# The last tile of scores in PSUM banks of its own, and the last output in half chunks over two queues

## The chip, the cores and the metric

One core of one Trainium2 chip runs the whole kernel. The metric is device time in microseconds (us), from start to end of one execution. The kernel before took 549.41 us (median of 3 runs, 548.23 to 549.83).

In the profile's rows PE is the matrix engine (PEld its weight loads), DVE the vector engine, ACT the scalar engine, POOL the GpSimd engine, and SP the engine that does nothing but issue transfers. SPq and ACTq are the sequencers that issue DMA transfers for SP and ACT.

## The reference

A graph attention layer over 16 graphs of 512 nodes with 512 features. `v` holds the nodes, `q` a condition vector per graph, `adj` an integer mask with 11 labels. Cut to what matters:

```python
vcq = concat([v, q_exp], -1)                   # q_exp is 0 in rows whose sum is 0
self_feat = vcq @ W_self.T + b_self            # 16 x 512 x 512
output = self_feat
for d in range(2):                             # the mask, and the mask transposed
    A = (adj if d == 0 else swapaxes(adj, 1, 2))[:, :, :20]
    bias = A @ w_bias + b_bias                 # 512 nodes x 20 keys
    qh, kh = heads(self_feat @ Wq[d].T + bq[d]), heads(self_feat[:, :20] @ Wk[d].T + bk[d])
    aff = where(A.sum(-1) > 0, qh . kh / sqrt(32), NEG) + bias     # 16 heads
    w = softmax(aff, -1)                       # over the 20 keys
    out_t = einsum('bnhm,bmf->bnhf', w, self_feat[:, :20])
    output += einsum('bnhf,hgf->bnhg', out_t, Wout[d]) + bout[d]
return v + relu(output)
```

Everything is float32. The kernel holds node features transposed, features on the partitions and nodes along the columns, and returns `out` as 16 x 512 features x 512 nodes; the host turns it back.

## The kernel before, in words

**Stages.** A setup (keys, folded weights, values) is followed by one round per graph, b = 0 to 15. The order of all instructions is written out by hand, and each engine runs its own in that order. A round computes the self features of the next graph, the scores of this one, and the output of the one before, so PE always has something to do. The last graph has no successor, and its work is written out below the loop: this is the tail, from about 515 us on, and only its last 10 us change.

**Scores.** For one graph there are four tiles of scores, (c, l): l is the half of the nodes (256 of them), c says which heads. A tile has 4 groups of 64 nodes, and for each group 4 heads x 40 numbers (2 directions x 20 keys) on each of two halves of the partitions. The last tile is (1, 1). It is computed in two parts, i = 0 and 1, of two groups each, so that the softmax of part 0 runs while PE computes part 1. Part i has a PSUM bank of its own, `ps_e0` or `ps_e1`. A part goes through: maximum and subtraction (DVE, `weigh_plain`, L463 and L465), exponential (ACT, L468), sum and reciprocal (DVE, `total_part`, L474 and L475), multiplication by the reciprocal (`normal_part`, L479; part 0 on POOL, part 1 on DVE) and a transposition in blocks of 32 (`turn_part`, L482, DVE) into `wt`, from where PE multiplies it with the values.

**Output.** The output of a graph gathers in four PSUM banks, `outsum[b][0..3]`. The 512 output features are four chunks of 128: chunk 2p + c. Banks 2p and 2p + 1 hold chunks 2p (c = 0, columns 0 to 255) and 2p + 1 (c = 1, columns 256 to 511); of the nodes the first of the two banks has the even blocks of 32, the second the odd ones. Banks 0 and 1 are one tile (`ps_o15_s1`), banks 2 and 3 another (`ps_o15_s0`). They start with the self features (`seed_out`, ACT, L556), and `attend` (L569) adds weights x values with `start=False`. A span (c, lo, hi) of `attend` names the half of the columns and the groups lo to hi - 1 of the 8 groups of 64 nodes; for each span and bank there are 6 matmuls, 4 with 32 and 2 with 64 output rows. Spans with c = 0 need only the tiles (0, 0) and (0, 1); (1, 0, 4) needs the tile (1, 0); (1, 4, 6) needs part 0 of the last tile, and (1, 6, 8) part 1.

`end` turns a chunk into output: relu and the node features `x` added. On DVE one instruction per bank does both (L611, 128 x 256); on ACT it is the relu alone (L613, 128 x 512 for both banks), and `add_rows` (L619) adds `x` on POOL or DVE. `send` (L1362) stores a chunk, 128 rows of 2 KB, 256 KB. An engine waits for the last instruction that another engine has, ahead in the code, on the same tile, even where the two touch different columns.

**The end of the tail before.** After `attend` of all (0, 0, 8) and of (1, 0, 4) in banks 0 and 1, ACT does the relu of chunks 2 and 0 (c = 0). POOL adds `x` to chunk 2, SP stores it. PE goes on with (1, 0, 6) in banks 2 and 3 and (1, 4, 6) in banks 0 and 1. DVE finishes part 1 of the last tile, then adds `x` to chunk 0, SP stores it. PE does (1, 6, 8) in all banks, and then DVE does `end` of chunks 3 and 1, each stored whole by SP. The reciprocals of part 1 are written into unused columns of `ps_e1`, a PSUM bank.

Of the kernel before, what the change touches and what calls it, by code (L numbers as in the profile page):

```python
# [7 lines left out]
F32 = mybir.dt.float32  # L8
# [5 lines left out]
P = 128  # L14
# [4 lines left out]
def gat_kernel(  # L19
# [449 lines left out]

    def total_part(b, c, l, i):  # L470
        f = weighs[b, c, l][:, bass.ts(i, 2)].rearrange("p g (h m) -> p (g h) m", m=NG)
        sm = soft.tile([P, per // 2], F32, tag="sm", name=f"sm{b}_{c}{l}{i}")
        smalls[i] = terms[c, l][i][:, 0, bass.ds(HL * S, per // 2)] if i else sm
        nc.vector.tensor_reduce(sm, f, AX.X, ALU.add)  # L474
        nc.vector.reciprocal(smalls[i], sm)  # L475

    def normal_part(b, c, l, i, engine):
        f = weighs[b, c, l][:, bass.ts(i, 2)].rearrange("p g (h m) -> p (g h) m", m=NG)
# [78 lines left out]
            outsum[b][a].rearrange("p (c n r) -> p c n r", c=2, r=R), spread_out(sfs[b], a), AF.Copy  # L557
        )

    def attend(b, spans=((0, 0, 2 * HL), (1, 0, 2 * HL)), banks=range(HL)):  # L560


        vd = vds[b].rearrange("p c e i g -> p c (e i g)")
        pairs, ones = ((1, 2, 1), (5, 2, 3)), ((0, 1, 0), (3, 1, 2), (4, 1, 2), (7, 1, 4))
        runs = (ones, spans[:1]), (pairs, spans), (ones, spans[1:])
        for c, lo, hi, at, n, j in [(*span, *of) for group, those in runs for span in those for of in group]:
            for a in banks:
                r = bass.ts(a, R)
                nc.tensor.matmul(  # L569
                    outsum[b][a][bass.ds(at // 2 * DH, n * DH), bass.ds(c * N // 2 + lo * R, (hi - lo) * R)].rearrange(  # L570
                        "p (n r) -> p n r", r=R
                    ),
                    vd[r, c, bass.ds(at * DH, n * DH)],
                    wts[b][r, c].rearrange("p l (g w) -> p (l g) w", g=HL)[:, lo:hi, bass.ts(j, 32)],
                    start=False, stop=n == 1 + (c == 0), skip_group_check=True,
                )
# [26 lines left out]
    def end(b, p, c, engine, us=slice(0, 2)):  # L603
# [5 lines left out]
        if engine is nc.vector:  # L609
            for u in range(us.stop - us.start):  # L610
                nc.vector.scalar_tensor_tensor(to[:, u], ps[:, u], 0.0, of[:, u], ALU.max, ALU.add)  # L611
        elif engine is nc.scalar:
            nc.scalar.activation(to, ps, AF.Relu)  # L613
        else:
            engine.tensor_add(to, to, of)

    def add_rows(b, p, c, engine):
        to = outt[b][:, 2 * p + c]
        engine.tensor_add(to, to, xs[b][:, 2 * p + c])  # L619

    def store(b, cs, ins=None):
        for c in cs:
            behind(nc.sync.dma_start(out[b, bass.ts(c, P)], outt[b][:, c]), ins)
# [451 lines left out]
    with tc.manual_schedule():  # L1075
# [275 lines left out]
        normal_part(b, 1, 1, 0, nc.gpsimd)  # L1351
        add_rows(o, 1, 1, nc.gpsimd)
        store(o, (3,))
        weigh_plain(b, 1, 1, 1)
        turn_part(b, 1, 1, 0)
        attend(b, ((0, 0, 8),))
        attend(b, ((1, 0, 4),), range(2))
        spare = const.tile([P, C, WD], F32, tag="g", name=f"o{b}", bufs=1).rearrange("p c w -> p (c w)")
        outt[b] = spare[:, : C * N].rearrange("p (c n) -> p c n", c=C)

        def send(queue, c):
            queue.dma_start(out[b, bass.ts(c, P)], outt[b][:, c])  # L1362

        for p in (1, 0):
            end(b, p, 0, nc.scalar)
        add_rows(b, 1, 0, nc.gpsimd)
        send(nc.sync, 2)
        attend(b, ((1, 0, 6),), range(2, 4))
        attend(b, ((1, 4, 6),), range(2))
        total_part(b, 1, 1, 1)  # L1370
        normal_part(b, 1, 1, 1, nc.vector)
        turn_part(b, 1, 1, 1)
        add_rows(b, 0, 0, nc.vector)
        send(nc.sync, 0)
        attend(b, ((1, 6, 8),))
        for p in (1, 0):
            end(b, p, 1, nc.vector)
            send(nc.sync, 2 * p + 1)


# [44 lines left out]
```

## Time and profile before

| | |
|---|---|
| time, median of 3 | 549.41 us |
| time of the profiled execution | 548.23 us |
| its span, first to last instruction | 546.2 us |
| busy in the span: PE, DVE, ACT, POOL | 99%, 88%, 74%, 80% |
| last matmul ends | 541.37 us |
| last DVE instruction ends | 542.82 us |
| last store issued | 542.84 us |
| DMA engines fall idle | 544.4 us |

2.0 us of the time lie outside the span. A row of the timeline has start and duration in us, engine, line and operation, output <- input with shapes, and in brackets for how long the engine was idle before and who ended that. Rows that follow each other are merged (x2). A row of stage windows has the stretch in us, its length, the busy time of PE, PEld, DVE, ACT and POOL with counts, then the granted PE clock, the busy share of the 16 DMA engines, and GB/s. In the profile each float32 matmul stands as two records.

### The profile page before, as it was taken

The numbers are of one execution on the slowest core, as the hardware profiler recorded it, in microseconds if no ns is written. First come the engines' busy times: TensorE is split into PE (matmuls) and PEld (weight loads), VectorE is DVE, ScalarE is ACT, GpSimd is POOL, SyncE is SP. The second block draws the span as 40 slices with busy tenths as digits, with TensorE's granted clock in tenths as the row PEclk, the third lists the DMA queues.
The fourth block names the chain that finished last, engine by engine and source line by source line (L and its number), as shares of the span: only waits on it lengthen the run. The fifth ranks groups of instructions, "written<-read, shape, count | busy, mean of one in ns | idle before, by whom it ended". The sixth has DMA issues, their size and how long they took to land.

```text
span 546.2 us, 19673 instructions
## 1 busy us (share of the span) xinstructions
PE 540.2 (99%) x7932; PEld 423.7 (78%) x7932; DVE 481.3 (88%) x711; ACT 404.1 (74%) x999; POOL 434.3 (80%) x418
## 2 busy tenths in 40 slices
PE   9999999999999999999999999999999999999996
PEld 6544368889888878787888878887878788878784
DVE  1776678889999999999989999999999999999997
ACT  1225435888887979788888888888878787978664
POOL 2637996779979797979798888888897979797664
PEclk9999999999999999999999999999999999999998
DMA  8999999978886877878776758676777777736034
GB/s 306 377 396 355 314 360 342 311 259 251 226 255 190 250 194 225 227 217 233 220 219 192 236 180 232 203 231 188 231 210 210 194 230 191 240 92 200 2 116 156
DMA packets 100546, 126.45 MB, mean 232 GB/s; under 512 B 19608, under 2 KB 68694, under 8 KB 98408
## 3 DMA queue, kind: packets, MB, share of 16 engines
q1 hardware_dynamic: 98856, 122.19, 72.2%
q0 software_dynamic: 1168, 2.23, 1.8%
q8 instruction: 62, 1.02, 0.8%
q10 hardware_dynamic: 432, 0.79, 0.4%
q14 instruction: 28, 0.23, 0.1%
HBM read 86.23 MB, written 40.24 MB: 232 GB/s over the span
## 4 chain that ended last, share of the span: by engine, by line
PE 97%; DVE 2%; ACT 0%; issue 0%; DVEq 0%
PE ps_f L667 32%; PE ps_a L397 24%; PE ps_c L397 11%; PE ps_d L397 6%; PE ps_o_f L569 5%; PE ps_v L893 3%; PE ps_k L831 3%; PE ps_kv L781 2%; PE ps_a L284 1%; PE ps_o_c L569 1%; PE ps_l L397 1%; PE ps_c L284 1%; PE ps_warm L737 1%; PE ps_o_s L569 0%; DVE o L611 0%; DVE w L465 0%
## 5 line engine op out<-in xcount | busy, mean ns | idle before, releaser
L327 ACT ACTIVATE prod<-adj,wb_sb 128x80 f32<-128x80 int32 x330 | 116.0, 429 | 0.0
L537 POOL TENSOR_TENSOR w<-w,sm 128x640 f32<-128x640 f32 x63 | 80.3, 1275 | 33.0 <-DVE sm L533 29.3
L667 PE MATMUL ps_f<-t,ws_s 128*64 128x246 f32 x720 | 80.0, 370 | 0.0
L667 PEld LDWEIGHTS ps_f<-t,ws_s 128*64 128x64 f32 x720 | 51.7, 136 | 18.9
L528 ACT ACTIVATE w<-w 128x640 f32<-128x640 f32 x60 | 43.9, 731 | 18.0 <-DVE w L524 18.0
L545 DVE STREAM_TRANSPOSE wt<-w 128x640 f32<-128x640 f32 x63 | 52.5, 834 | 0.1
L667 PE MATMUL ps_f<-x,ws_v 128*64 128x246 f32 x480 | 52.4, 371 | 0.0
L532 DVE TENSOR_REDUCE sm<-w 128x32 f32<-128x640 f32 x63 | 51.1, 811 | 1.1 <-ACT w L528 0.8
L523 DVE TENSOR_REDUCE ps_d<-w 128x32 f32<-128x640 f32 x59 | 48.7, 826 | 1.8 <-ACT ps_d L431 0.2
L524 DVE TENSOR_TENSOR w<-w,ps_d 128x640 f32<-128x640 f32 x59 | 48.4, 821 | 2.0
L370 POOL TENSOR_TENSOR k<-g,k 128x608 f32<-128x608 f32 x30 | 44.8, 1492 | 0.0
L667 PEld LDWEIGHTS ps_f<-x,ws_v 128*64 128x64 f32 x480 | 34.7, 137 | 13.0
L397 PEld LDWEIGHTS ps_a<-g,sf 128*64 128x64 f32 x544 | 34.2, 137 | 5.9 <-issue 5.8
L397 PE MATMUL ps_a<-g,sf 128*64 128x152 f32 x544 | 38.6, 295 | 0.0
L397 PE MATMUL ps_d<-g,sf 128*64 128x152 f32 x544 | 37.9, 293 | 0.0
L346 ACT COPY both<-add 64x80 f32<-64x80 f32 x128 | 32.6, 254 | 5.7 <-DVE add L338 4.6
L569 PE MATMUL ps_o_c<-wt,vd 32*32 32x256 f32 (+1 forms) x720 | 36.8, 386 | 0.0
L338 DVE TENSOR_REDUCE add<-prod 128x80 f32<-128x960 f32 x32 | 36.7, 1146 | 0.0
L682 POOL TENSOR_TENSOR t<-x,t 128x492 f32<-128x492 f32 x30 | 34.9, 1163 | 1.2
L397 PEld LDWEIGHTS ps_d<-g,sf 128*64 128x64 f32 x544 | 35.3, 137 | 0.2 <-ACT sf L685 0.2
L333 POOL TENSOR_SCALAR prod<-cond 128x80 f32<-128x80 f32 x32 | 18.1, 566 | 21.7 <-DVE cond L332 20.2
L569 PE MATMUL ps_o_f<-wt,vd 32*32 32x256 f32 (+1 forms) x672 | 34.6, 386 | 0.0
(300 smaller groups left out, 1435.8 us busy)
## 6 DMA issues: line engine op xcount, KB each, us to landing
g<-g_d SPq DMA_DIRECT2D x60, 304.0 KB
g_d<-st SPq DMA_DIRECT2D x16, 1064.0 KB
out_T<-o SPq DMA_DIRECT2D x64, 256.0 KB
x<-in_xT SPq DMA_DIRECT2D x56, 256.0 KB
xn<-in_xn SPq DMA_DIRECT2D x48, 256.0 KB
adj<-in_adj SPq DMA_DIRECT2D x52, 220.0 KB
vd<-bd_d SPq DMA_DIRECT2D x64, 64.0 KB
nz<-nz_d SPq DMA_DIRECT2D x14, 256.0 KB
```

The lines of the kernel that those rows point to most:

```text
L327: nc.scalar.activation(p[:, :, l], a[:, :, l], AF.Identity, scale=wb_sb[:, l : l + 1])
L338: done["masks"] = nc.vector.tensor_reduce(add, prods.pop((b, h)), AX.X, ALU.add)
L370: done["ksum"] = engine.tensor_sub(to, one, two)
L397: nc.tensor.matmul(slot(g)[bass.ts(p, P // 2), : HL * S].rearrange("p (h m) -> p h m", m=NG)[:, :, 1:], of(k)[:, bass.ds(first + g * P // ...
L523: nc.vector.tensor_reduce(mx, f, AX.X, ALU.max)
L524: done["weigh"] = (engine or nc.vector).tensor_sub(f, f, mx.unsqueeze(2).to_broadcast([P, per, NG]))
L528: done["exp"] = nc.scalar.activation(t, t, AF.Exp)
L532: nc.vector.tensor_reduce(sm, heads(weighs[b, c, l]), AX.X, ALU.add)
L537: done["normal"] = nc.gpsimd.tensor_mul(f, f, smalls.pop((b, c, l)).unsqueeze(2).to_broadcast([P, per, NG]))
L545: done["turn"] = nc.vector.transpose(wts[b][:, c, l], weighs.pop((b, c, l)).rearrange("p g w -> p (g w)"))
L569: nc.tensor.matmul(outsum[b][a][bass.ds(at // 2 * DH, n * DH), bass.ds(c * N // 2 + lo * R, (hi - lo) * R)].rearrange("p (n r) -> p n r", ...
L667: nc.tensor.matmul(parts[b][n in (2, 3, 5)][bass.ts(a, P // 2), bass.ts(i, HN)], lhs, x[:, k], start=False, stop=k == 1, skip_group_check= ...
```

## The change

Only the end of the tail changes (the line numbers after it shift by up to 21).

- Three further PSUM tiles, four banks, are taken for the last graph: `c` (two banks), `f0` and `f1`. `f0` and `f1` are the banks in which parts 0 and 1 of the last tile of scores lay. In each, the 128 columns of c = 1 and groups 4 to 7 are seeded with self features (`seed_groups`, ACT, L620, four instructions of 128 x 128), three ahead of the exponential of part 1 and one behind it.
- The spans (1, 4, 6) and (1, 6, 8) go to these banks (`base=HL`), for all four banks at a time. All of (1, 0, 4) now goes with (0, 0, 8) in one call of `attend`, ahead of ACT's relu.
- Since `f1` is the bank `ps_e1`, the reciprocals of part 1 no longer go there: they stay in SBUF (`sm`).
- `x` is added to chunk 0 on POOL, behind chunk 2, and no longer on DVE.
- Chunks 3 and 1 are finished in halves of 256 nodes (`end_groups`, DVE, L625, eight instructions of 128 x 128 in place of four of 128 x 256): groups 0 to 3 from the old banks, groups 4 to 7 from the new ones.
- Six stores in place of four. ACT's queue: the first half of 3, the first half of 1, the second half of 1. SP's queue: chunk 2 whole, the second half of 3, chunk 0 whole. A half is 128 rows of 1 KB.

```diff
     def total_part(b, c, l, i):
-        sm = soft.tile([P, per // 2], F32, tag="sm", name=f"sm{b}_{c}{l}{i}")
-        smalls[i] = terms[c, l][i][:, 0, bass.ds(HL * S, per // 2)] if i else sm
+        sm = smalls[i] = soft.tile([P, per // 2], F32, tag="sm", name=f"sm{b}_{c}{l}{i}")
         nc.vector.tensor_reduce(sm, f, AX.X, ALU.add)
-        nc.vector.reciprocal(smalls[i], sm)
+        nc.vector.reciprocal(sm, sm)
...
-    def attend(b, spans=((0, 0, 2 * HL), (1, 0, 2 * HL)), banks=range(HL)):
+    def attend(b, spans=((0, 0, 2 * HL), (1, 0, 2 * HL)), banks=range(HL), first=0, base=0):
...
-        runs = (ones, spans[:1]), (pairs, spans), (ones, spans[1:])
+        runs = ((ones, spans[:1]), (pairs, spans), (ones, spans[1:]), (ones, spans[:1]))[first : first + 3]
...
+    def columns(bank, c, lo, hi):
+        return bank[:, bass.ds(c * N // 2 + lo * R, (hi - lo) * R)].rearrange("p (n r) -> p n r", r=R)
+
+    def seed_groups(b, a, c, lo, hi):
+        nc.scalar.activation(
+            columns(outsum[b][HL + a], c, lo, hi), spread_out(sfs[b], a)[:, c, lo:hi], AF.Copy
+        )
+
+    def end_groups(b, a, c, lo, hi, bank):
+        nc.vector.scalar_tensor_tensor(
+            spread_out(outt[b], a)[:, c, lo:hi], columns(bank, c, lo, hi), 0.0, spread_out(xs[b], a)[:, c, lo:hi],
+            ALU.max, ALU.add,
+        )
...
+        new_outs(b, ((accs, "c"), (accs, "f0")))
+        for a in range(3):
+            seed_groups(b, a, 1, 4, 8)
         weigh_plain(b, 1, 1, 1)
+        new_outs(b, ((accs, "f1"),))
+        seed_groups(b, 3, 1, 4, 8)
         turn_part(b, 1, 1, 0)
-        attend(b, ((0, 0, 8),))
-        attend(b, ((1, 0, 4),), range(2))
...
+        attend(b, ((0, 0, 8), (1, 0, 4)))
         for p in (1, 0):
             end(b, p, 0, nc.scalar)
         add_rows(b, 1, 0, nc.gpsimd)
-        send(nc.sync, 2)
-        attend(b, ((1, 0, 6),), range(2, 4))
-        attend(b, ((1, 4, 6),), range(2))
+        add_rows(b, 0, 0, nc.gpsimd)
+        attend(b, ((1, 4, 6),), base=HL)
         total_part(b, 1, 1, 1)
         normal_part(b, 1, 1, 1, nc.vector)
         turn_part(b, 1, 1, 1)
-        add_rows(b, 0, 0, nc.vector)
+        attend(b, ((1, 6, 8),), first=1, base=HL)
+        send(nc.sync, 2)
+        for p in (1, 0):
+            for a in (2 * p, 2 * p + 1):
+                end_groups(b, a, 1, 0, 4, outsum[b][a])
+            send(nc.scalar, 2 * p + 1, slice(0, N // 2))
+        for p, queue in ((1, nc.sync), (0, nc.scalar)):
+            for a in (2 * p, 2 * p + 1):
+                end_groups(b, a, 1, 4, 8, outsum[b][HL + a])
+            send(queue, 2 * p + 1, slice(N // 2, N))
         send(nc.sync, 0)
-        attend(b, ((1, 6, 8),))
-        for p in (1, 0):
-            end(b, p, 1, nc.vector)
-            send(nc.sync, 2 * p + 1)
```

How the instructions stand on three engines. `o15` is the last graph's output tile, `sf15` its self features, `x15` its node features; in brackets are the engines (or DMA semaphores) whose work an instruction waits for.

ACT from the last seed of the old banks on, before:

```order
L556 ACTIVATE ps_o15_s0_7398<-sf15_6856 128x512 [waits Activation_49]
L468 ACTIVATE w15_11_7421<-w15_11_7421 128x320 [waits DVE_49]
L613 ACTIVATE o15_7475<-ps_o15_s0_7398 128x2x8x32 [waits DMAHW0_49,PE_49,Activation_49]
L613 ACTIVATE o15_7475<-ps_o15_s1_7384 128x2x8x32 [waits PE_49]
L1421 UNCONDITIONAL_BRANCH
```

and now:

```order
L555 ACTIVATE ps_o15_s0_7398<-sf15_6856 128x512 [waits Activation_49]
L620 ACTIVATE ps_o15_c_7434<-sf15_6856 128x128 [waits Activation_49] x2
L620 ACTIVATE ps_o15_f0_7435<-sf15_6856 128x128 [waits PE_49]
L468 ACTIVATE w15_11_7421<-w15_11_7421 128x320 [waits DVE_49]
L620 ACTIVATE ps_o15_f1_7443<-sf15_6856 128x128 [waits PE_49]
L612 ACTIVATE o15_7446<-ps_o15_s0_7398 128x2x8x32 [waits DMAHW0_49,PE_49]
L612 ACTIVATE o15_7446<-ps_o15_s1_7384 128x2x8x32
L1378 DMA out_T<-o15_7446 128x256 [waits DMAHW7_49,DVE_49]
L1378 DMA out_T<-o15_7446 128x256 [waits DMAHW0_49,DVE_49]
L1378 DMA out_T<-o15_7446 128x256 [waits DMAHW3_49,DVE_49]
```

Four seeds came in around the exponential L468 and three stores behind the relus. The first relu's wait for PE was for the 24th matmul of the tail's `attend` (the last one of (0, 0, 8)); since (1, 0, 4) for all banks now stands in the same call, it is for the 48th.

DVE from the reciprocal of part 1 on, before:

```order
L475 RECIPROCAL ps_e1_7306<-sm15_111_7504 128x16 [waits DVE_49]
L479 TENSOR_TENSOR w15_11_7421<-w15_11_7421,ps_e1_7306 128x320 [waits DVE_49]
L482 STREAM_TRANSPOSE wt15_7357<-w15_11_7421 128x320 [waits DVE_49]
L619 TENSOR_TENSOR o15_7475<-o15_7475,x15_6526 128x512 [waits DMAHW0_49,Activation_49]
L611 SCALAR_TENSOR_TENSOR o15_7475<-ps_o15_s0_7398,x15_6526 128x8x32 [waits PE_49]
L611 SCALAR_TENSOR_TENSOR o15_7475<-ps_o15_s0_7398,x15_6526 128x8x32
L611 SCALAR_TENSOR_TENSOR o15_7475<-ps_o15_s1_7384,x15_6526 128x8x32 x2
```

and now:

```order
L474 RECIPROCAL sm15_111_7523<-sm15_111_7523 128x16 [waits DVE_49]
L478 TENSOR_TENSOR w15_11_7421<-w15_11_7421,sm15_111_7523 128x320 [waits DVE_49]
L481 STREAM_TRANSPOSE wt15_7357<-w15_11_7421 128x320 [waits DVE_49]
L625 SCALAR_TENSOR_TENSOR o15_7446<-ps_o15_s0_7398,x15_6526 128x4x32 [waits DMAHW0_49,Activation_49]
L625 SCALAR_TENSOR_TENSOR o15_7446<-ps_o15_s0_7398,x15_6526 128x4x32
L625 SCALAR_TENSOR_TENSOR o15_7446<-ps_o15_s1_7384,x15_6526 128x4x32 [waits Activation_49]
L625 SCALAR_TENSOR_TENSOR o15_7446<-ps_o15_s1_7384,x15_6526 128x4x32
L625 SCALAR_TENSOR_TENSOR o15_7446<-ps_o15_f0_7435,x15_6526 128x4x32 [waits PE_49]
L625 SCALAR_TENSOR_TENSOR o15_7446<-ps_o15_f1_7443,x15_6526 128x4x32 [waits PE_49]
L625 SCALAR_TENSOR_TENSOR o15_7446<-ps_o15_c_7434,x15_6526 128x4x32 x2
```

The addition L619 is gone from DVE, the multiplication L479 (now L478) reads its reciprocals from SBUF, and only the last four finishing instructions wait for PE's last matmuls.

SP's last stores, before and now:

```order
L1362 DMA out_T<-o15_7475 128x512 [waits DMAHW6_49,Pool_49]
L1362 DMA out_T<-o15_7475 128x512 [waits DMAHW7_49,DVE_49]
L1362 DMA out_T<-o15_7475 128x512 [waits DMAHW0_49,DVE_49]
L1362 DMA out_T<-o15_7475 128x512 [waits DMAHW1_49,DVE_49]
```

```order
L1378 DMA out_T<-o15_7446 128x512 [waits DMAHW6_49,Pool_49]
L1378 DMA out_T<-o15_7446 128x256 [waits DMAHW1_49,DVE_49]
L1378 DMA out_T<-o15_7446 128x512 [waits DMAHW2_49,Pool_49]
```

They were chunks 2, 0, 3, 1; they are chunk 2, the second half of 3, and chunk 0, which now waits for POOL and stands last.

More of the change, by code (lines that the diff above doesn't have):

```diff
@@ L569, in attend @@
                 nc.tensor.matmul(
-                    outsum[b][a][bass.ds(at // 2 * DH, n * DH), bass.ds(c * N // 2 + lo * R, (hi - lo) * R)].rearrange(
+                    outsum[b][base + a][bass.ds(at // 2 * DH, n * DH), bass.ds(c * N // 2 + lo * R, (hi - lo) * R)].rearrange(
                         "p (n r) -> p n r", r=R
@@ L1353, in gat_kernel, with send @@
         store(o, (3,))
+        new_outs(b, ((accs, "c"), (accs, "f0")))
+        for a in range(3):
+            seed_groups(b, a, 1, 4, 8)
         weigh_plain(b, 1, 1, 1)
+        new_outs(b, ((accs, "f1"),))
+        seed_groups(b, 3, 1, 4, 8)
         turn_part(b, 1, 1, 0)
-        attend(b, ((0, 0, 8),))
-        attend(b, ((1, 0, 4),), range(2))
         spare = const.tile([P, C, WD], F32, tag="g", name=f"o{b}", bufs=1).rearrange("p c w -> p (c w)")
         outt[b] = spare[:, : C * N].rearrange("p (c n) -> p c n", c=C)
-        def send(queue, c):
-            queue.dma_start(out[b, bass.ts(c, P)], outt[b][:, c])
+        def send(queue, c, at=slice(0, N)):
+            queue.dma_start(out[b, bass.ts(c, P), at], outt[b][:, c, at])
+        attend(b, ((0, 0, 8), (1, 0, 4)))
         for p in (1, 0):
```

## The prediction

> **What bounds the kernel now.** I read the page first, then the chain of waits at the end, the timeline of the last 9 us engine by engine, and stage windows for the DMA engines.
>
> ```profile
> PE 540.2 (99%) x7932; PEld 423.7 (78%) x7932; DVE 481.3 (88%) x711; ACT 404.1 (74%) x999; POOL 434.3 (80%) x418
> PE 97%; DVE 2%; ACT 0%; issue 0%; DVEq 0%
> ```
>
> PE is the bound over nearly the whole span, but the change touches nothing ahead of 536 us, so only the tail counts. The chain there ends so:
>
> ```profile
> 537.97 0.27 ACT w L468
> 538.23 0.11 issue
> 538.34 0.59 ACT o L613
> 538.93 0.04 issue
> 538.98 2.40 PE ps_o_s L569 x85
> 541.37 0.02 issue
> 541.40 0.42 DVE o L611
> 541.82 0.33 DVEq L1421
> 542.15 0.66 DVE o L611 x2
> ```
>
> ACT's relu releases PE at 538.98, PE's last matmul releases DVE at 541.40, and DVE needs 1.42 us for the two last chunks. DVE and SP:
>
> ```profile
> 538.99 0.26 DVE L475 RECIPROCAL ps_e<-sm 128x16 f32<-128x16 f32 x1
> 539.29 0.49 DVE L479 TENSOR_TENSOR w<-w,ps_e 128x320 f32<-128x320 f32 x1
> 539.81 0.51 DVE L482 STREAM_TRANSPOSE wt<-w 128x320 f32<-128x320 f32 x1
> 540.25 0.72 DVE L619 TENSOR_TENSOR o<-o,x 128x512 f32<-128x512 f32 x1
> 541.40 1.42 DVE L611 SCALAR_TENSOR_TENSOR o<-ps_o_s,x 128x256 f32<-128x256 f32 x4 [0.43 <-PE ps_o_s L569]
> 540.44 0.33 SPq L1362 DMA_DIRECT2D out_T<-o  x1
> 540.99 0.33 SPq L1362 DMA_DIRECT2D out_T<-o  x1
> 542.18 0.33 SPq L1362 DMA_DIRECT2D out_T<-o  x1
> 542.84 0.33 SPq L1362 DMA_DIRECT2D out_T<-o  x1
> ```
>
> The chain stops at DVE's end, but the span goes on for 3.4 us with stores:
>
> ```profile
> 541.25:542.65 1.40, 0.08 (x8) 0.00 (x0) 1.25 (x4) 0.00 (x0) 0.00 (x0) 0.57 0.97 369
> 542.65:543.00 0.35, 0.00 (x0) 0.00 (x0) 0.17 (x1) 0.00 (x0) 0.00 (x0) 0.50 0.08 24
> 543.00:544.40 1.40, 0.00 (x0) 0.00 (x0) 0.00 (x0) 0.00 (x0) 0.00 (x0) 0.50 0.97 372
> 544.40:546.20 1.80, 0.00 (x0) 0.00 (x0) 0.00 (x0) 0.00 (x0) 0.00 (x0) 0.50 0.01 2
> ```
>
> The four last stores (1.05 MB) go through the DMA engines in two stretches of two, each at a share of 0.97. 0.97 of 1.40 us is 1.36 us for two stores, 0.68 us for each of 256 KB; so the stretches begin at about 541.27 and 543.02, 0.83 us after 540.44 and 542.18, the issues that open them, and between them the engines stand still for only 0.38 us. From the last byte to the end of the span it is 1.8 us. So the end is set by when the last megabyte can enter the DMA engines, and they are nearly full already from 541.27 on.
>
> **The change, part by part.** Sums are made against the profiled execution: span 546.2, time 548.23; its span ends 1.8 us after its last byte.
>
> *Seeds.* ACT has four more instructions. Neighbours:
>
> ```profile
> L613 ACT ACTIVATE o<-ps_o_c 128x256 f32<-128x256 f32 x1 | 0.4, 364 | 0.0
> L613 ACT ACTIVATE o<-ps_o_s 128x512 f32<-128x512 f32 x4 | 2.3, 592 | 0.2 <-PE ps_o_s L569 0.2
> L468 ACT ACTIVATE w<-w 128x320 f32<-128x320 f32 x2 | 0.9, 470 | 1.3 <-DVE w L465 1.3
> ```
>
> From 256 to 512 columns it is 228 ns, so a 128 x 128 seed is about 0.25 us. Three of them, 0.75 us, lie in the 1.3 us that ACT waits for DVE ahead of the second exponential: nothing. Without that cover each would put its 0.25 us on the chain. The fourth ends at about 538.6, ahead of its user.
>
> *PE and the relus.* The work has the same columns, with 96 matmuls in place of 84. What is new is the order: ACT's first relu now waits for all 48 matmuls of the first `attend`. Before, the first 36 ended at 538.89:
>
> ```profile
> 538.07 0.82 PE L569 MATMUL ps_o_s<-wt,vd 32*32 32x128 f32 x24
> 538.75:539.00 0.25, 0.16 (x12) 0.03 (x4) 0.21 (x2) 0.22 (x2) 0.25 (x1) 1.00 0.00 0
> 539.95 1.24 PEld L569 LDWEIGHTS ps_o_s<-wt,vd 32*32 32x32 f32 x72 [0.28 <-issue]
> 540.49 0.21 PEld L569 LDWEIGHTS ps_o_s<-wt,vd 32*32 32x32 f32 x28
> ```
>
> The twelve more go to banks 2 and 3, whose rows of the array stood idle in that stretch. Between 538.89 (all beside the others) and 539.54 (all behind them, at two thirds of the 0.97 us that twelve matmuls of 192 columns took, from 538.98 in the chain to the next weight loads at 539.95) I take 539.0, because four banks at a time is how `attend` runs elsewhere. The relus then run 539.05 to 540.23, not 538.34 to 539.55: the wait of PE for ACT is gone, and ACT waits for PE in its place. The span (1, 4, 6) follows on PE until about 539.9. The last span waits for the transposition of part 1, which ended at 540.32, and starts at about 540.4; before, it took from its weight loads at 540.49 to 541.37, so PE ends at about 541.3: gain 0.1 us.
>
> *POOL.* Behind the relus come two additions of
>
> ```profile
> L619 POOL TENSOR_TENSOR o<-o,x 128x512 f32<-128x512 f32 x3 | 3.8, 1274 | 0.0
> 537.92 2.50 POOL L619 TENSOR_TENSOR o<-o,x 128x512 f32<-128x512 f32 x2
> ```
>
> The first starts at 539.05 + 0.59 + 0.02 = 539.66 (before, 539.15 behind another) and ends at 540.93; the second at 542.2. So chunk 2 is stored at 540.97 in place of 540.44, and chunk 0, which DVE had ready at 540.97, at 542.24 in place of 540.99. This is what the change pays.
>
> *DVE.* L619 (0.72) goes. The starts of L611 lie 0.34 us apart for 256 columns at 0.42 us each; with 128 columns less (0.13 us) a half costs 0.28 us, 0.20 from start to start. Four run from 540.25 to 541.13, beside PE's last span; four from 541.3 to 542.18, where L611 ended at 542.82.
>
> *Stores.* On ACT's queue: 3 first half at 540.77, 1 first half at 541.17, 1 second half at 542.22; on SP's: chunk 2 at 540.97, 3 second half at 541.82, chunk 0 at 542.24. An issue there costs a little more than SP's 0.33, with nothing behind it on ACT but the next store:
>
> ```profile
> L740 ACTq DMA_DIRECT2D ws_v<-in_wsT x3: 409/453/458, 0.7 to 1.7; - x3
> ```
>
> With 0.83 us to the first byte, the first stretch begins at 541.6 in place of 541.27, and 1.05 MB at 385 GB/s (369 over a share of 0.97) need 2.72 us: with no gap the last byte is out at 544.3. Nothing is gained by the earlier last issue (542.24 for 542.84), since the queue is full when it comes: 3a, 2, 1a, 3b take it to 543.3, and chunk 0 with 1b to 544.3. The gap of 0.38 us is filled, and 0.33 us of that is spent on the later start.
>
> The Trainium skill, "DMA: Bandwidth & Descriptors", section "Issuing engines are not separate DMA queues", says that transfers issued from several engines interleave on the same 16 DMA engines, and that this saves issue time only. By that rule the second queue gives no more than the issue times above, as my sum has it; the trace's share of 0.97 with SP's queue alone agrees.
>
> Halves have rows of 1 KB. The trace has such rows only in loads of the values, where the share was lower too:
>
> ```profile
> 523.00:526.25 3.25, 3.25 (x55) 3.25 (x52) 3.08 (x6) 2.26 (x4) 2.39 (x3) 1.00 0.56 160
> ```
>
> 160 over 0.56 is 286 GB/s: 0.46 us for a half in place of 0.34. Bounds for the last byte: 544.3 and, four halves later, 544.8. They are stores, like the 385, but with the rows of the 286; I take the middle, 544.5. With 544.4 before, **the sum is +0.1 us**: span 546.3, profiled time 548.3, and on the median 549.5.
>
> **The rivals.**
>
> *The multiplication stops behind POOL (slower).* L479 gets its second input from SBUF, no longer from PSUM. The trace has one pair of that kind:
>
> ```profile
> L524 DVE TENSOR_TENSOR w<-w,ps_d x59: 820/820/822, 96.7 to 511.4; 128x640 f32<-128x640 f32 x59
> L524 DVE TENSOR_TENSOR w<-w,mx x1: 1609/1609/1609, 517.7 to 517.7; 128x640 f32<-128x640 f32 x1
> 517.73 1.61 DVE L524 TENSOR_TENSOR w<-w,mx 128x640 f32<-128x640 f32 x1
> 517.11 1.55 POOL L440 TENSOR_TENSOR full<-cq,both 128x640 f32<-128x640 f32 x1 [0.89 <-DVE add L338]
> ```
>
> With both inputs in SBUF it stood still until POOL's instruction ended (517.11 + 1.55 = 518.66) and took 0.68 us from there. If POOL has begun its addition of chunk 2 by 539.28, the multiplication waits till about 540.42, and all of DVE and PE behind it comes 1.13 us later: the last finishing instruction ends at 543.3, the last half is issued at 543.35, and its byte is out at 544.7 to 545.2, +0.3 to +0.8 us; if POOL wins a second time, 1.27 more, +2.0. It decides where PE's 48 matmuls end by 538.62. They can't: 36 of them ended at 538.89, and POOL is free from 539.17 till 539.66, in which the multiplication (539.29 to 539.78) gets through. Time 549.9, up to 551.4.
>
> The Trainium skill, "SBUF — State Buffer", section "Who interferes with whom", states this as a rule: a DVE instruction with two SBUF inputs contends with a GpSimd instruction that reads SBUF, and issue order decides who blocks. By that rule alone the change would lose; the trace agrees with the rule (1609 ns for 820), and the order of the releases decides here.
>
> *The stores flow better than one queue's rate (faster).* With six stores at hand from two queues the rate may rise to the best that a stage of the trace shows:
>
> ```profile
> 45.00:46.00 1.00, 1.00 (x17) 0.64 (x16) 0.51 (x2) 0.00 (x0) 1.00 (x1) 1.00 1.09 424
> ```
>
> 424 GB/s make it 2.47 us from 541.6, and the last byte is out at 544.07, which chunk 0's own path (542.24 + 0.83 + 0.68 = 543.75) allows: -0.33 us, and if chunk 0 bounds, -0.65. For it: the gap closes. Against it: the share of 0.97 already.
> Time 548.8 to 549.1.
>
> *PE's pause slows the last matmuls.* PE now idles from 539.9 to 540.4, and the windows above show the granted clock at 0.50 as soon as PE had nothing to do. At half the clock the last span could take up to 0.9 us more, but DVE's last two halves would then be issued by 543.1, and their bytes follow at 543.9 to 544.3: hidden by the queue, +0.0 to +0.2. Time 549.5.
>
> **How the numbers follow.** No change in the sum, between -0.1 and +0.4 us: 0.55, with PE's clock 0.10 more; faster stores 0.25; the blocked multiplication 0.10. In a whole of 549 us 0.3% is 1.6 us, about what a measurement of this kernel can tell from no change. Only POOL winning twice reaches that on the slow side (0.03), and nothing on the fast side does by more than the scatter of the medians (0.03 for that): same 0.94. The predicted time is 549.5; the range takes in -0.65 and +0.8 and the scatter of the runs shown (548.23 to 549.83), which is wider than all terms: 548.3 to 550.4.
>
> **What would show it.** PE no longer waits for ACT's relu; the last span starts at 540.4 behind the transposition. L478 lasts 0.49, not 1.2 or more. POOL's additions end near 540.9 and 542.2, and chunk 0's store is the last on SP. The eight halves on DVE last 0.28 us. The DMA engines are busy without a gap from 541.6 to 544.3 or later. I am wrong where the last byte is out before 544.0, where it comes after 544.9, or where L478 is long.

## The result: 0.22% slower, and the profile after

The changed kernel took 550.28 us (median of 22 runs, 548.82 to 551.43), the kernel before 549.21 us (22 runs, 548.16 to 550.41). The ratio is 1.0022 with a 95% interval from 1.0015 to 1.0029: 0.8 to 1.6 us, inside the 0.3% that I had called too little to tell, yet clear of no change, and not the 0.1 us of my sum.

The two profiled executions differ by 2.3 us in their spans (546.2 and 548.5), but not all of that is the change. One instruction that both kernels have, DVE's last sums, shows it (timelines of DVE; start, length, line, operation):

```profile
538.47 0.49 DVE L474 TENSOR_REDUCE sm<-w 128x16 f32<-128x320 f32 x1
```

```profile
539.10 0.49 DVE L473 TENSOR_REDUCE sm<-w 128x16 f32<-128x320 f32 x1
```

The first row is of before, the second of the changed kernel: 0.63 us had been lost ahead of the changed code. DVE's 101st instruction already started 0.63 us later (83.05 and 83.68), and its 691st too (533.37 and 534.00), so the difference arises in the first 83 us and then stays. Two executions of one kernel differ there in the same way. So all times below are counted from the start of these last sums, written as +x; that leaves the tail alone: 7.70 us to the end of the span before, 9.44 us after.

The timeline of the changed kernel's tail, DVE, ACT, POOL and the two store queues:

```profile
539.60 1.08 ACT L612 ACTIVATE o<-ps_o_s 128x512 f32<-128x512 f32 x2 [0.36 <-PE ps_o_s L568]
539.91 0.49 DVE L478 TENSOR_TENSOR w<-w,sm 128x320 f32<-128x320 f32 x1
540.28 2.49 POOL L632 TENSOR_TENSOR o<-o,x 128x512 f32<-128x512 f32 x2 [0.45 <-ACT o L612]
540.43 0.51 DVE L481 STREAM_TRANSPOSE wt<-w 128x320 f32<-128x320 f32 x1
540.87 0.85 DVE L625 SCALAR_TENSOR_TENSOR o<-ps_o_s,x 128x128 f32<-128x128 f32 x4
541.35 2.32 ACTq L1378 DMA_DIRECT2D out_T<-o  x3
541.57 2.17 SPq L1378 DMA_DIRECT2D out_T<-o  x3
542.39 0.49 DVE L625 SCALAR_TENSOR_TENSOR o<-ps_o_f,x 128x128 f32<-128x128 f32 x2 [0.67 <-PE ps_o_f L568]
542.79 0.48 DVE L625 SCALAR_TENSOR_TENSOR o<-ps_o_c,x 128x128 f32<-128x128 f32 x2
```

Less 0.63, the relu starts at 538.97, POOL's two additions run from 539.65 to 542.14, and the first stores go out at 540.72 and 540.94: the prediction had 539.05, 539.66 to 542.2, 540.77 and 540.97. Only DVE's second group of halves is late, at 541.76 in place of 541.3. What the prediction did not have stands at the end of the stores. Stage windows of the same profile (length, the engines' busy times, granted clock, share of the 16 DMA engines, GB/s):

```profile
542.20:543.70 1.50, 0.02 (x3) 0.00 (x0) 0.88 (x4) 0.00 (x0) 0.56 (x1) 1.00 0.97 341
543.70:545.40 1.70, 0.00 (x0) 0.00 (x0) 0.00 (x0) 0.00 (x0) 0.00 (x0) 0.94 0.88 307
545.40:546.77 1.37, 0.00 (x0) 0.00 (x0) 0.00 (x0) 0.00 (x0) 0.00 (x0) 0.50 0.07 24
546.77:548.50 1.73, 0.00 (x0) 0.00 (x0) 0.00 (x0) 0.00 (x0) 0.00 (x0) 0.50 0.00 0
```

The stores run full until 545.4, +6.3. Then a share of 0.07, about one engine of 16, works on alone for 1.37 us at 24 GB/s, and the span's end waits for it. The DMA queues of the window from 542 to 547 say what that engine had to do besides:

```profile
q1 hardware_dynamic: 432, 0.66, 36.0%
q10 hardware_dynamic: 432, 0.39, 23.7%
q8 instruction: 1, 0.02, 1.1%
```

One packet of 16 KB of instructions: the block of PE's code that the rest of this document is about. In the page of the whole span, queue 8 has 63 packets after and 62 before. PE's rows there grew with it: 7956 products and as many weight loads, for 7932 and 7932, 48 instructions more. The single records of the trace around the packet (start and length in us, queue, bytes; no engine stands in them, but down to the block each begins 6 to 18 ns behind the end of the one above it):

```
542.826 0.154 q1   2048
542.986 0.154 q1   2048
543.146 0.154 q1   2048
543.306 0.154 q1   2048
543.466 0.154 q1   2048
543.638 0.192 q1   2048
543.839 0.879 q8  16384
   (the same engine's next records cannot be told from those of the others)
545.432 0.046 q1   1024
   (from here only one packet at a time is under way)
546.595 0.084 q1   2048
546.681 0.084 q1   2048
```

Elsewhere in these stores 2 KB mostly take 0.082 to 0.087 us and 1 KB 0.046. That these are the records of the engine that lags is read from how closely they follow each other, and from the sum: the six packets ahead of the block lost 0.07 to 0.11 us each, 0.45 together, and the block held the engine for 0.88 us: 1.3 us, about what this engine is behind the others.

### The profile page after: what moved, and what is told of

Read it like the earlier page. It is cut to its first block, busy times and chain, and to the rows that moved or that the text cites. A ratio compares the mean times of both kernels' runs of the same rounds, so it can differ in the third digit from the quotient of the medians.

```text
span 548.5 us, 19732 instructions
## 1 busy us (share of the span) xinstructions
PE 539.8 (98%) x7956; PEld 423.8 (77%) x7956; DVE 481.0 (88%) x714; ACT 404.9 (74%) x1003; POOL 435.6 (79%) x419
## 4 chain that ended last, share of the span: by engine, by line
PE 94%; POOL 2%; DMA 1%; ACT 1%; DVE 1%; issue 1%; DVEq 0%; POOLq 0%; ACTq 0%
PE ps_f L680 32%; PE ps_a L397 24%; PE ps_c L397 11%; PE ps_d L397 6%; PE ps_o_f L568 5%; PE ps_k L844 3%; PE ps_kv L794 2%; PE ps_o_c L568 2%; PE ps_v L906 1%; PE ps_a L284 1%; DMA cq_d<-c 1%; PE ps_l L397 1%; PE ps_c L284 1%; PE ps_warm L750 1%; POOL rx L217 0%
## 5 line engine op out<-in xcount | busy, mean ns | idle before, releaser
L568 PE MATMUL ps_o_c<-wt,vd 32*32 32x256 f32 (+3 forms) x768 | 38.4, 376 | 0.8 <-DVE wt L481 0.8
L568 PE MATMUL ps_o_f<-wt,vd 32*32 32x256 f32 (+3 forms) x720 | 36.3, 376 | 0.3 <-issue 0.3
```

Of the source, the lines that this page charges most:

```text
L568: nc.tensor.matmul(outsum[b][base + a][bass.ds(at // 2 * DH, n * DH), bass.ds(c * N // 2 + lo * R, (hi - lo) * R)].rearrange("p (n r) -> p ...
```

## The experiments

**First look for the cause: move the block, leave the tail as it is.** PE's code comes in blocks (63 packets of 16 KB over the run), so instructions added at the start of the program move the place of each block in the rest. The kernels warm PE up with 7 products that nothing reads; these are replaced. In the changed kernel:

```diff
-            for _ in range(7):
+            for _ in range(2):
                 nc.tensor.matmul(warm[:, :P], ones, ones, start=True, stop=True)
+            for k in range(56):
+                r = bass.ts(k % 4, 32)
+                nc.tensor.matmul(warm[r, :16], ones[r, :32], ones[r, :16], start=True, stop=True)
```

> The changed kernel with 204 more PE instructions at its very start (2 of the 7 warm-up products stay, 56 tiny ones of 32 x 16 come behind them; nothing reads them). Theory (code block): the changed kernel's 48 more PE instructions make the 63rd block of 16 KB of PE's code, and it comes over a DMA engine at 543.84, in the midst of the last stores; with 204 more instructions ahead of the tail the same block comes some 3 us earlier, before the first of the last stores has data. Then still 63 blocks, no trickle of 25 GB/s behind the stores, the last byte about 1.4 us earlier against PE's end, and a time about 1.0 us below that of the changed kernel plus what the start costs, that is within 0.4 us of the kernel before with the same start (b_code_early). Rival (the end comes from what the change does on the engines: PE's last span 0.5 us late, half-chunk stores, two queues): the start moves nothing in the tail, the trickle stays, and the time stays 1.1 us above b_code_early.

Windows of its stores and of what follows:

```profile
542.85:545.90 3.05, 0.04 (x3) 0.00 (x0) 0.88 (x4) 0.00 (x0) 0.60 (x1) 0.57 0.94 344
545.90:547.60 1.70, 0.00 (x0) 0.00 (x0) 0.00 (x0) 0.00 (x0) 0.00 (x0) 0.50 0.00 0
```

There are still 63 blocks, but the last lay at +0.26 to +1.53, ahead of these stores. The engine that worked on alone is gone, the last byte is out at +6.18 in place of +7.66, and the tail is 7.79 us in place of 9.44. Every instruction of the tail is the same. In time it was 1.0013 of before (1.0002 to 1.0024), with a start that cost 0.8 us in this execution (DVE's sixth instruction began at 15.05, in the changed kernel at 14.25) and 1.4 to 1.8 us in the three other profiles with the same start.

The same start in the kernel before is the control (b_code_early), and 13 of the tiny products with 6 of the 7 wide ones make its PE stream as long as the changed kernel's (b_code_late).

> The kernel before with the same 204 more PE instructions at its start: the control for the start's own cost. Theory: the 63rd block is there, but ahead of the last stores, no trickle; the time is that of the kernel before plus the start, estimated at -1 to +3 us from 5 products of 0.24 us per pass less and 112 short passes more. Rival (any 63rd block costs, wherever it falls): at least +1.0 us, with the tail of before unchanged in all else.

> The kernel before with 48 more PE instructions at its start (one warm-up product less, 13 tiny ones more), so that its PE stream is as long as the changed kernel's. Theory (code block): a 63rd block appears, is fetched some 2 to 3 us after PE's last work is dispatched, at about 543, and holds one of the 16 DMA engines for 0.9 us (with slow packets ahead of it 1.4 us) in the last two stores: time +0.8 to +1.4 us on the kernel before, about 550.2, as slow as the changed kernel without any of its edits. Rival (engines and stores of the change): no difference, within 0.3 us.

b_code_early: block at +0.29 to +1.31, last byte +5.96, tail 7.60, ratio 1.0005 (0.9995 to 1.0016): the theory's side. With the same start the two kernels' tails differ by 0.19 us. Their medians, 550.17 and 549.62 us, differ by 0.55 where at most 0.4 was expected; the two intervals overlap. b_code_late missed: its 63rd block came only at +8.21, behind the span (+7.84), though its PE stream is as long as the changed kernel's. So the length alone does not put the block into the stores. It was 1.0018 of before (1.0005 to 1.0031) all the same, a median of 550.25 us: the theory's number without its mechanism, in the one execution that was profiled. Its tail does not show why; in its profile 1.5 us are lost between 43 and 83 us, where the other profiles differ from the first by 0.0 to 0.7. Where the block falls in the executions without a profile is not known, for this kernel or any other, and this stays unexplained.

**One rival by itself: the reciprocal in SBUF.** The kernel before with only that part of the change:

```diff
-        sm = soft.tile([P, per // 2], F32, tag="sm", name=f"sm{b}_{c}{l}{i}")
-        smalls[i] = terms[c, l][i][:, 0, bass.ds(HL * S, per // 2)] if i else sm
+        sm = smalls[i] = soft.tile([P, per // 2], F32, tag="sm", name=f"sm{b}_{c}{l}{i}")
         nc.vector.tensor_reduce(sm, f, AX.X, ALU.add)
-        nc.vector.reciprocal(smalls[i], sm)
+        nc.vector.reciprocal(sm, sm)
```

> The kernel before with one edit of the change alone: the reciprocal of the last sums is kept in SBUF, so that the last multiplication on DVE has two SBUF inputs while POOL is adding (537.92 to 540.42). Theory: the multiplication, 0.49 us in the kernel before, stops behind POOL's second addition and ends near 540.7 to 540.9 in place of 539.78; everything behind it comes about 1.1 us later, time +0.9 to +1.3 us. Rival (no such stop; the 1609 ns of the one pair in the trace had another reason): multiplication stays at 0.5 to 0.7 us, time within 0.3 us. In the changed kernel it lasted 0.49 us because POOL was free.

Its timeline of DVE and POOL:

```profile
538.41 2.50 POOL L618 TENSOR_TENSOR o<-o,x 128x512 f32<-128x512 f32 x2
539.48 0.25 DVE L474 RECIPROCAL sm<-sm 128x16 f32<-128x16 f32 x1
539.77 1.49 DVE L478 TENSOR_TENSOR w<-w,sm 128x320 f32<-128x320 f32 x1
541.29 0.51 DVE L481 STREAM_TRANSPOSE wt<-w 128x320 f32<-128x320 f32 x1
```

1.49 us in place of 0.49: with both inputs in SBUF the multiplication stood still until POOL's second addition ended (538.41 + 2.50 = 540.91). The rival's mechanism and its price (1.13 us predicted, 1.00 measured) are right. In the changed kernel the multiplication lasts 0.49 us, because POOL is free between 539.83 and 540.28 and it starts at 539.91, 0.08 us behind POOL's last instruction. This kernel was 1.0015 of before (1.0004 to 1.0025), with a tail of 9.35 us, 1.65 more than before. The stop put the last store 0.91 us later; the rest again goes with a block, here at +4.04 to +5.30, behind which one engine works on alone for 0.65 us, with no PE instruction added.

**Is it chance, and does it go the other way?** Both kernels were profiled again unaltered; the kernel before got 96 more PE instructions (4 wide products, 27 tiny); and the changed kernel lost its 7 warm-up products, 28 PE instructions less.

> The changed kernel, unaltered, profiled a second time, to see whether the block of PE's code comes at the same place in every execution. Tail = from the start of DVE's last sums (539.10 in the changed kernel's first profile, 538.47 in that of before) to the span's end: 9.4 us there, 7.7 us in the kernel before. Theory (place set by the number of PE instructions alone): 63rd block again some 2 us behind the start of PE's last span, tail 9.2 to 9.6. Rival (the block comes by chance, as the median, 1.1 us over before and not 1.7, would allow): tail either 9.4 or about 7.8.

> The kernel before, unaltered, profiled a second time. Theory (number of PE instructions alone): 62 blocks in the span, tail 7.7 again. Rival (by chance): a 63rd block in the last stores in some executions, since the kernel before with only its reciprocal moved had one at 543.0 with no PE instruction more: tail 9.

> The kernel before with 96 more PE instructions at its start (48 more brought the 63rd block to 548.3, behind the span; 204 more to 540.65, ahead of the last stores). Theory (number of instructions): between the two, the block falls into the last four stores, one DMA engine ends 0.9 to 1.4 us behind the other 15, tail 8.6 to 9.2 in place of 7.7. Rival (the block comes only where PE waits over 1 us ahead of its last span, as in the changed kernel and with the reciprocal moved): no block in the last stores, tail 7.7.

> The changed kernel without its 7 warm-up products at the start, which nothing reads: 28 PE instructions fewer, 20 more than the kernel before. Theory (number of instructions): the 63rd block is asked for 28 instructions later, which lie behind PE's last work, so it comes behind the span, as with the 48 more in the kernel before; no engine lags, tail 7.8 to 7.9. Rival (PE's wait brings it): block in the last stores, tail 9.4.

a_again repeats the tail: block at +4.72 (+4.74 the first time), then one engine alone for 1.40 us, last byte +7.65, tail 9.30:

```profile
541.60:544.70 3.10, 0.00 (x0) 0.00 (x0) 0.88 (x4) 0.00 (x0) 0.57 (x1) 0.50 0.96 332
544.70:546.10 1.40, 0.00 (x0) 0.00 (x0) 0.00 (x0) 0.00 (x0) 0.00 (x0) 0.50 0.07 25
546.10:547.80 1.70, 0.00 (x0) 0.00 (x0) 0.00 (x0) 0.00 (x0) 0.00 (x0) 0.50 0.00 0
```

It is no accident of one execution. b_again had no block in the stores either; its tail was 7.99, because PE paused for 0.37 us among its last weight loads (see the end). In a_code_fewer the block came at +10.06, behind the span, no engine worked on alone, the last byte was out at +6.22 and the tail was 7.80. But the time had 2.92 us outside the span, where the changed kernel has 1.8: in this one execution it looks as if the block that had left the stores was paid for behind them.

In b_code_mid the block lay at +2.37 to +3.25, across the first byte of the last stores (+2.8 in the kernel before); the tail of 7.97 is near neither number that I gave. The lag is there, but further ahead: the second store's issue on SP takes 1.09 us, 0.33 in the kernel before, and for 0.6 us one engine works alone between the first store and the rest (SP's timeline and a stage window):

```profile
542.23 1.09 SPq L1365 DMA_DIRECT2D out_T<-o  x1
543.20:543.80 0.60, 0.00 (x0) 0.00 (x0) 0.60 (x3) 0.00 (x0) 0.00 (x0) 0.50 0.08 24
```

So a block just ahead of the stores can go with a longer issue of the next one (b_early_cheap, below, shows it again); how it comes to that is not shown. Most of the lost time is made up here, where the last three stores run in one stretch.

**The two terms of the sum that could still be wrong**, both on the start of a_code_early: PE's last span in the other order, and all six stores on one queue.

```diff
-        attend(b, ((1, 6, 8),), first=1, base=HL)
+        attend(b, ((1, 6, 8),), base=HL)
```

> As a_code_early (the changed kernel with 204 more PE instructions at its start, so that no code block falls into the last stores), with PE's last span in the order of the kernel before: the products of one 32-column group first, the pairs of 64 columns behind them. In a_code_early that span went from 541.69 to DVE's start on it at 542.94, 1.25 us, with a pause of 0.47 us between the weight loads of the last pair and its neighbour; in the kernel before the whole last span took 0.9 us. Theory (the order of the two kinds costs the pause): about 0.95 us, the last stores are issued 0.3 us earlier, tail 7.5 to 7.7 in place of 7.8. Rival (the pause comes with the 1.1 us wait ahead of it, whatever the order): span 1.2 us, tail 7.8.

```diff
-            send(nc.scalar, 2 * p + 1, slice(0, N // 2))
+            send(nc.sync, 2 * p + 1, slice(0, N // 2))
-        for p, queue in ((1, nc.sync), (0, nc.scalar)):
+        for p, queue in ((1, nc.sync), (0, nc.sync)):
```

> As a_code_early, with all six last stores on SP's queue. Theory (a second queue saves issue time only): six issues on SP at about 0.55 us from one to the next in place of three on each queue; the last goes out at +5.0 to +5.3 us from the start of DVE's last sums in place of +4.1, the last byte 0.2 to 0.6 us later than +6.2, tail 8.0 to 8.4. Rival (two queues also raise the rate of the DMA engines): tail over 8.6, with the share of the DMA engines below 0.9 where data is at hand. Rival (issue is hidden behind the DMA engines): tail 7.8.

a_ones_first: the span did take 1.0 us in place of 1.25, the last store was issued at +3.84 in place of +4.09, and the last byte was out at +6.16 in place of +6.18. Being earlier on PE gained nothing: the tail is 7.76, the rival's 7.8. a_one_queue: its queue and the stage windows of its stores,

```profile
543.59 2.79 SPq L1381 DMA_DIRECT2D out_T<-o  x6
```

```profile
544.40:545.40 1.00, 0.01 (x1) 0.00 (x0) 0.88 (x4) 0.00 (x0) 0.39 (x1) 1.00 0.96 350
545.40:546.40 1.00, 0.00 (x0) 0.00 (x0) 0.00 (x0) 0.00 (x0) 0.00 (x0) 0.50 0.92 305
546.40:547.60 1.20, 0.00 (x0) 0.00 (x0) 0.00 (x0) 0.00 (x0) 0.00 (x0) 0.50 0.89 324
```

Six issues lie 0.48 us apart on average; the last goes out at +4.85, the last byte at +6.59, and the tail is 8.13. The second queue is worth 0.34 us to this change, but not all of that is issue time. Chunk 2, which waits for POOL, now stands first in the only queue, ahead of a half that is ready, so the first store goes out at +2.47 in place of +2.25: 0.22 us by the order alone. The share of the DMA engines stays at 0.89 to 0.96 with one queue, so the rest is small gaps between the issues, and hardly the rate.

**The change with no block in its stores, at no cost at the start.** 40 tiny products now come first, and 5 of the 7 wide ones behind them, so that the start lasts as long as it did (DVE's sixth instruction at 14.10 and 14.16; 14.08 in the kernel before, 14.25 in the changed one); in both kernels.

> The changed kernel with the same start as b_early_cheap: the change without a code block in the last stores, against the kernel before without one. Theory: 9.55 to 9.6 us from the start of the last sums to the very end, 0.1 to 0.3 us more than b_early_cheap (my sum had +0.1), and about 1.5 us less than the changed kernel (11.2 and 11.1). Rival (the change itself costs the 1.2 us of the medians): 1 us more than b_early_cheap.

> The kernel before with 152 more PE instructions at its start, placed so that the start lasts as long as it did (40 tiny products of 32 x 16 ahead of 5 of the 7 warm-up products). Theory: the code block lies ahead of the last stores, and time from the start of the last sums to the very end is about 9.4 us, where the kernel before had 9.8 and 10.1 (7.7 and 8.0 in the span, 2.06 behind it): -0.3 to -0.5 us, plus -0.2 to +0.5 for the start: time -0.5 to +0.2 us against before. Rival (the block costs nothing in the kernel before): 0 to +0.5.

a_early_cheap: block at +0.71 to +1.59, its stores without an engine left alone, last byte +6.17, tail 7.78:

```profile
542.30:545.35 3.05, 0.00 (x0) 0.00 (x0) 0.58 (x3) 0.00 (x0) 0.58 (x1) 0.87 0.97 344
545.35:547.00 1.65, 0.00 (x0) 0.00 (x0) 0.00 (x0) 0.00 (x0) 0.00 (x0) 0.50 0.00 0
```

Its time was 549.05 us, 1.0000 of before, with an interval from 0.9991 to 1.0009 that does not meet that of the changed kernel (1.0015 to 1.0029). In b_early_cheap the block came where I had not expected it, at +1.65 to +3.51, and 1.86 us long. It fell into the stores of the kernel *before*, and that kernel then shows the same lag:

```profile
543.60:545.40 1.80, 0.00 (x0) 0.00 (x0) 0.00 (x0) 0.00 (x0) 0.00 (x0) 0.79 1.00 378
545.40:546.00 0.60, 0.00 (x0) 0.00 (x0) 0.00 (x0) 0.00 (x0) 0.00 (x0) 0.50 0.08 27
546.00:547.70 1.70, 0.00 (x0) 0.00 (x0) 0.00 (x0) 0.00 (x0) 0.00 (x0) 0.50 0.00 0
```

Here, too, the issue of the second store took longer, 1.36 us:

```profile
541.44 1.36 SPq L1365 DMA_DIRECT2D out_T<-o  x1
```

Last byte +7.11, tail 8.77, ratio 1.0009 (0.9995 to 1.0022). So the block costs either kernel when it meets the last stores; this pair gives no control, and b_code_early remains the one.

All tails together, in order of where the 63rd block was seen (times in us from the start of the last sums, the time outside the span from the profiled execution's own time; a_again, b_again, b_code_mid, a_code_fewer, a_ones_first and a_one_queue ran once each, for their profile):

| kernel | PE instructions beyond before | 63rd block | last byte | end of span | time outside the span | sum |
|---|---|---|---|---|---|---|
| before | 0 | not seen | +6.05 | 7.70 | 2.06 | 9.76 |
| b_again | 0 | not seen | +6.34 | 7.99 | 2.06 | 10.05 |
| a_code_early | 252 | +0.26 to 1.53 | +6.18 | 7.79 | 1.77 | 9.56 |
| a_ones_first | 252 | +0.28 to 1.26 | +6.16 | 7.76 | 1.78 | 9.54 |
| b_code_early | 204 | +0.29 to 1.31 | +5.96 | 7.60 | 1.77 | 9.37 |
| a_one_queue | 252 | +0.30 to 1.62 | +6.59 | 8.13 | 1.78 | 9.91 |
| a_early_cheap | 200 | +0.71 to 1.59 | +6.17 | 7.78 | 1.78 | 9.56 |
| b_early_cheap | 152 | +1.65 to 3.51 | +7.11 | 8.77 | 1.86 | 10.63 |
| b_code_mid | 96 | +2.37 to 3.25 | +6.32 | 7.97 | 1.84 | 9.80 |
| b_sums_sbuf | 0 | +4.04 to 5.30 | +7.62 | 9.35 | 1.77 | 11.12 |
| a_again | 48 | +4.72 to 5.60 | +7.65 | 9.30 | 1.78 | 11.08 |
| after | 48 | +4.74 to 5.62 | +7.66 | 9.44 | 1.78 | 11.22 |
| b_code_late | 48 | +8.21 to 9.40 | +6.11 | 7.84 | 1.78 | 9.62 |
| a_code_fewer | 20 | +10.06 to 10.96 | +6.22 | 7.80 | 2.92 | 10.71 |

The sums of the two unaltered kernels, 11.22 and 11.08 against 9.76 and 10.05, differ by 1.25 us on the mean: that is the 1.07 us of the medians, within its interval.

## Why the prediction was wrong

**The step that failed** is *Stores*: "with no gap the last byte is out at 544.3", and the bounds of 544.3 and 544.8 with it, gave all 16 DMA engines to the stores. On the clock of before the last byte came at 546.1, behind the 544.9 that was named as a sign of being wrong. What the runs showed in its place is one more transfer among them, a 16 KB block of PE's code at +4.74, which left one engine 1.4 us behind. Without it the change's last byte is out at +6.17 to +6.22 (three kernels), with it at +7.65 and +7.66.

Behind it stands a term that *PE and the relus* put at nothing: "The work has the same columns, with 96 matmuls in place of 84." I weighed these products as columns and as an order, and not as instructions that have to be brought. The view was there before the change: the page's queue 8, instruction, with its packets, and the count of PE's rows beside it. From the first to the last of the 62 blocks of the kernel before, 61 steps, PE ran 15,608 instructions in the trace (products, weight loads and waits), 256 to a block. Where 96 or more instructions were added, the 63rd block begins when PE has started 16,096 to 16,160 of them, about 63 x 256 = 16,128. The kernel before ends with 16,088, 40 short of that, the changed one with 16,136. So near the edge the count alone does not place the block; the last section comes back to that.

The Trainium skill, "Runtime: NRT & Kernel Launch", section "Instruction fetch mechanics", says that an engine's instructions are streamed in 16 KiB blocks of 256 instructions over a DMA queue of the sequencer's own, and that crossing a block costs little and is mostly hidden. The blocks agree with this trace (16,384 bytes, 256 instructions). One that falls among the last stores is not hidden: 1.5 to 1.7 us (tails 9.44 and 9.30 against 7.79 and 7.78). What the blocks that fall into the work cost, no run here measures.

**A smaller error: what lies around the span.** I added 2.03 us to every span. It was 2.06 in the kernel before, 1.77 to 1.86 in all the kernels whose block lies in the span or shortly behind it, and 2.92 where it came 2.3 us behind it. That 0.3 us comes back to the change. Why the kernel before has 2.06 stays open: the traces of b_code_late and a_code_fewer hold the packet that came behind their span, and those of the kernel before hold none.

**The terms of the sum, one by one.**

- *Relu, POOL, first stores*: within 0.1 us everywhere, as the rows after show.
- *PE's last span*: it started at +1.90 as predicted (540.37 on the clock of before, 540.4 predicted) and took 1.39 us where I had 0.9. The chain of waits of the changed kernel has the place:

```profile
541.00 0.27 PE ps_o_c L568 x2
...
541.37 0.25 issue
541.62 0.27 PE ps_o_f L568 x2
```

  Two neighbouring weight loads start 0.53 us apart there. It moved the last issue from +3.71 (a_early_cheap, which has no such pause) to +4.23, and it cost nothing: a_early_cheap, without the pause, has its last byte at +6.17, and a_code_early, with it, at +6.18. That agrees with the prediction's point that the earlier last issue gains nothing since the queue is full when it comes; the size of 0.46 us was wrong.
- *Stores in halves*: predicted between 385 GB/s and the 286 of the loads with short rows, last byte at 544.3 to 544.8, taken 544.5. Without the block it is at 544.64 to 544.69 on the clock of before. A packet of 1 KB takes 0.046 us and one of 2 KB 0.084: halves cost a tenth more, not a third. The trace of before already had 1 KB packets at a median of 0.046 us; the 286 is the average of a window in which they took 0.055 us on the mean. The first byte came as predicted, at 541.58 in a_early_cheap; a tenth more on the halves makes 2.86 us from there, and the stretch took 3.06 at a share of 0.97. So the middle came close by luck, and the other 0.2 us, in gaps and slower packets, was not in the sum. (369 GB/s over 0.97 is 380, not 385, a slip worth 0.04 us.)
- *The sum*, +0.1 us in the span: 7.78 and 7.79 against 7.70, or against 7.60 with the same start. That agrees for what it counted, but it is not resolved: the second execution of the kernel before had 7.99, and its first had its last byte at 544.52, where I had read 544.4. a_early_cheap's 1.0000 (0.9991 to 1.0009) is what the change costs without the block, to about 0.5 us.

**The rivals.** The blocked multiplication did not come, for the reason given (the order of the releases), and b_sums_sbuf shows that it is real. The margin was thin: 0.08 us between POOL's end and the multiplication's start. The Trainium skill, "SBUF — State Buffer", section "Who interferes with whom", is borne out by it: 1.49 us against 0.49 with POOL at work and with POOL idle. The faster stores did not come: 344 GB/s over all of them at a share of 0.97. a_one_queue agrees with the rule of the Trainium skill, "DMA: Bandwidth & Descriptors", section "Issuing engines are not separate DMA queues", that the prediction had cited: a second queue gives issue time, at most 0.34 us here, and no rate. PE's slower clock left no mark on the end: a_early_cheap's last span took 0.87 us after the same wait. The loss I had not listed at all. The chances went to the terms that I could see on the engines, and none to a transfer that no line of the kernel issues.

## What to carry to other kernels

When a change adds instructions, count them as code as well: the page's instruction queues and the number of rows of each engine say how many make a block, and the place of the last block against the last transfers decides whether it costs time. Before a small loss is put down to the change itself, move the code by some unused instructions at the start and compare the tails from a common instruction on: here the 0.22% went away with every instruction of the change in place. And the end of a kernel is one DMA engine's end: a share of 1/16 with the others idle is the mark to look for.

## What the runs showed of the hardware that was not expected

- What puts the last block into the stores or behind them is settled only in part. With 96 or more added instructions it follows the count, and more of them by and large bring it earlier (the table). In the kernels that end within 40 instructions of 16,128 the count is not enough: 48 more put it at +4.74 in the changed kernel and at +8.21 in b_code_late, and b_sums_sbuf had one at +4.04 with none more, where the unaltered kernel before showed none. A wait of PE of 1.1 us ahead of its last span goes with it in the changed kernel and in b_sums_sbuf; but a_code_fewer has that wait too, and its block came at +10.06.
- PE paused for 0.37 to 0.65 us in its last span at one and the same place of its instruction stream, counted in the trace: behind instruction 16,066 in after, a_again, a_code_fewer and b_again, behind 16,322, 256 further, in a_code_early and a_one_queue. Kernels whose last span holds no such place (a_early_cheap, b_code_mid, b_code_early, b_early_cheap) have no pause over 0.2 us. Before, b_code_late, b_sums_sbuf and a_ones_first pass the place without one. 256 is the size of a block; that the change of block makes the pause is only a guess. In b_again it moved the last store and the span's end by 0.3 us; in the changed kernel it was hidden behind the stores.
- The two executions of each unaltered kernel differ by 0.25 us (before) and 0.6 us (after) ahead of the tail, all of it in the first 83 us. In all profiles the distance to the first one stays the same to 0.04 us from 163 us to the tail, 370 us in which PE sets the pace.
